# Two layer norms change engines, and the fourth block is turned one step sooner, where a mamba layer meets a linear layer

## The chip, the cores and the metric

The kernel runs on one core of one Trainium2 chip. The metric is the device time of one execution in microseconds (us). Five engines work beside each other, each on its own queue of instructions: TensorE (PE in the profile; its weight loads are PEld), VectorE (DVE), ScalarE (ACT), GpSimd (POOL) and SyncE (SP, which here issues nearly all DMA transfers). They meet through semaphores.

## The reference

Four sublayers work on x, which has 2048 tokens of 512 values. Each is added to x, and a layer norm over the 512 values follows.

```python
x = layernorm(x + mamba(x, W_in, conv, A_log, ..., W_out))   # gated scan, 16 heads of 64, state 16
x = layernorm(x + linear(x, weight, scale))     # x @ ternary weight * scale, row length bounded by tanh
x = layernorm(x + recurrent(x, w_y, w_x, conv, w_ig, w_ag, w_out))       # gelu branch times gated scan
x = layernorm(x + swiglu(x, gate, up, down))                             # 512 -> 2048 -> 512
# layernorm: (x - mean) / sqrt(var + 1e-5)
# linear: out = (x @ W) * scale; n = |out|; out *= tanh(n) / n; out *= min(0.99 / |out|, 1)
```

Everything is float32. In the linear layer the kernel writes each operand as a sum of two float32r pieces, so that one product becomes two faster ones.

## The kernel before

The tokens are worked in four blocks of 512 (`NBLK` = 4, `TB` = 512). A block lies in SBUF as `X[b]`, 128 partitions by four row groups j of 512 values. In the mamba layer the tiles of the four blocks share three buffers of the pool `outer`; block 3 gets the buffer of block 0.

The source is written as Python generators whose steps are woven together. The order of the source gives each instruction its priority; a scheduler then orders each engine's queue, taking the earliest instruction in the source that it believes ready. Each queue is strictly in order once it is made. `keep_in_program_order` holds one instruction behind all that its engine was given before it in the source.

**The end of mamba.** `conclude(3)` multiplies block 3 by `w_out` (L764), adds the result to `X[3]` (L779), calls `layernorm(X[b])` (L783) and stores the block to the DRAM tensor `x_mid` (L784, on SP). Its steps are woven with `linear(0)` and `linear(1)`. Then `first_layer.close` gives up the pool `outer`, and SP loads block 3 from `x_mid` into the tile that later layers use (L1002).

**The layer norm** (`layernorm`, L274 to L287). Its statistics are always on VectorE: `bn_stats` (L279), `bn_aggr` (L280), then a square root on ScalarE (L282) and a reciprocal (L283) on VectorE. Only the last part, four `tensor_scalar` over 128x512 (L285), one for each j, runs on the engine that is passed in. Before the change `conclude` gives VectorE for all blocks, and `linear` gives GpSimd for all blocks.

**The linear layer** (`linear(b)`) has four steps: turn the block with TensorE (L237), whose result ScalarE copies into the first piece `wu0` (L241) while VectorE makes the second piece `wd0` (L244); products of rows j = 0, 1 (L961, scaled on VectorE at L965); products of j = 2, 3; then the bound by tanh (L971 to L983), the addition to x (L985), the layer norm, and from block 1 on a store to `x_lin` (L254). There is one buffer for each piece, so a block can be turned into them only when the products of the block before it are done. For block 2 the copies of L241 are held in source order on ScalarE.

**The start of the recurrent layer.** `branches(0)` turns block 0 (L237), ScalarE copies it to `xT` (L248), and products with `w_x` (four, L1040) and `w_y` (four, L1040) follow. Its nine steps are woven with the eight of `linear(2)` and `linear(3)` by a plan that says how many of those follow each step. `xT` is a tile of the pool `rec`, which is opened on the same side of SBUF as `outer`, after `outer` is closed. In the compiled kernel `xT` takes bytes 151456 to 159648 of each partition, and `X[3]` of the mamba layer had bytes 153568 to 161760. ScalarE's first copy into `xT` therefore carries a wait for the store L784 to have landed.

Of the kernel before, what the change touches and what calls it, by code (L numbers as in the profile page):

```python
# [37 lines left out]
def model_kernel(ctx: ExitStack, tc: tile.TileContext, t: dict, out: bass.AP):  # L38
    nc = tc.nc
    ctx.enter_context(nc.allow_non_contiguous_dma(reason="small parameter columns"))  # L40
    BATCH, SEQ, _ = t["L0_attn_hidden_states"].shape
    NBLK = BATCH * SEQ // TB
# [17 lines left out]
    def bank(name):  # L60
        return ps.tile([P, 512], F32, tag="mm", name=name)
# [17 lines left out]
    def tokens():  # L79
        return op.tile([P, NJ, D], F32, tag="x", name="x", bufs=3)  # L80

    X = [tokens() for _ in range(3)]
# [170 lines left out]
    def store_rows(rows, x):  # L253
        nc.sync.dma_start(rows.rearrange("(j p) d -> p j d", p=P), x)  # L254
# [13 lines left out]
    def turn_blocks(dst, src=None, pinned=False):  # L268
        for k in range(NK):
            turned = nc.vector.transpose(dst[:, k, :], (src or dst)[:, k, :])  # L270
            if pinned:
                tc.keep_in_program_order(turned)

    def layernorm(x, n=NJ, engine=nc.vector):  # L274

        mv = sp.tile([P, NJ, 2], F32, tag="mv", name="mv")
        for j in range(n):
            st = sp.tile([P, 6], F32, tag="st", name="st", bufs=4)
            nc.vector.bn_stats(st, x[:, j, :])  # L279
            nc.vector.bn_aggr(mv[:, j, :], st)  # L280
        rs = sp.tile([P, NJ, 1], F32, tag="rs", name="rs")
        nc.scalar.activation(rs[:, :n], mv[:, :n, 1:2], AF.Sqrt, bias=eps)  # L282
        nc.vector.reciprocal(rs[:, :n], rs[:, :n])  # L283
        for j in range(n):
            engine.tensor_scalar(  # L285
                x[:, j, :], x[:, j, :], mv[:, j, 0:1], rs[:, j, :], ALU.subtract, ALU.mult
            )  # L287

    def causal_conv(acc, xpad, w, pinned=False):

        for k in range(3):
            tap = nc.vector.scalar_tensor_tensor(  # L292
                acc, xpad[:, k : k + TB], w[:, k : k + 1], acc, ALU.mult, ALU.add
            )
            if pinned and k == 0:
                tc.keep_in_program_order(tap)

    def weave(main, fill, plan, rest=True):

        for i, _ in enumerate(main):  # L300
            for _ in range(plan[i] if i < len(plan) else 0):
                next(fill, None)
        for _ in fill if rest else ():
            pass
# [451 lines left out]
    def conclude(b, st):  # L756


        xc, sums = st["xc"], st["sums"]
        rms = sp.tile([P, NJ], F32, tag="rms", name="rms")  # L760
        for j in range(NJ):
            po = bank("po")
            for m in range(NX):
                nc.tensor.matmul(  # L764
                    po, xc[:, m, j * P : (j + 1) * P], w_out[:, m, :],
                    start=(m == 0), stop=(m == NX - 1),
                )
                if m == NX // 2 - 1:
                    yield
            if j == 0:  # L770
                pss = bank("pss")
                for i in range(NJ):
                    nc.tensor.matmul(
                        pss[:, i : i + 1], sums[:, i * P : (i + 1) * P], ones,
                        start=True, stop=True,
                    )
                nc.scalar.activation(rms, pss[:, :NJ], AF.Sqrt, bias=eps, scale=1.0 / DI)
                nc.vector.reciprocal(rms, rms)
            nc.vector.scalar_tensor_tensor(  # L779
                X[b][:, j, :], po, rms[:, j : j + 1], X[b][:, j, :], ALU.mult, ALU.add  # L780
            )
            yield
        layernorm(X[b])  # L783
        nc.sync.dma_start(x_mid[b], X[b])  # L784

    def by_blocks(b, st):
# [4 lines left out]
    H, before, st = None, None, {}  # L791
# [10 lines left out]
    for b in range(NBLK):  # L802
# [19 lines left out]
        before, st = st, coming  # L822
# [43 lines left out]
    def later_layers(exact, last=None):  # L866
# [4 lines left out]
        X = Y  # L871
# [70 lines left out]
        def coming_block(b):  # L942

            x = ep.tile([P, NK, TB], F32, tag="lo", name=f"lin{b}" + suffix)
            load_blocks(x, x_lin[b])
            return x

        def linear(b):


            xT = transposed(
                ep, b, X, tags=("wu0", "wd0") if exact else ("wu0",), split=exact, behind=b == 2
            )
            yield
            o = ep.tile([P, NJ, D], F32, tag="wF", name="o" + suffix)
            ssq = sp.tile([P, NJ], F32, tag="ssq", name="ssq")
            for j in range(NJ):
                po = bank("po")
                for k in range(NK):
                    for x in xT:  # L960
                        nc.tensor.matmul(  # L961
                            po, x[:, k, j * P : (j + 1) * P], wf[:, k, :],
                            start=(k == 0 and x is xT[0]), stop=(k == NK - 1 and x is xT[-1]),
                        )
                nc.vector.tensor_tensor(o[:, j, :], po, f0s, ALU.mult)  # L965
                junk = ep.tile([P, GW], mybir.dt.bfloat16, tag="junk", name="junk2")
                nc.scalar.activation(junk, o[:, j, :], AF.Square, accum_out=ssq[:, j : j + 1])
                if j % 2:
                    yield
            norm = sp.tile([P, NJ], F32, tag="norm", name="norm")  # L970
            nc.scalar.activation(norm, ssq, AF.Sqrt)  # L971
            v = sp.tile([P, NJ], F32, tag="v", name="v")
            nc.vector.tensor_scalar(v, norm, 1e-7, None, ALU.max)
            f = sp.tile([P, NJ], F32, tag="f", name="f")
            nc.scalar.activation(f, v, AF.Tanh)
            nc.vector.tensor_scalar(v, v, 1e-7, None, ALU.add)
            nc.vector.reciprocal(v, v)
            nc.vector.tensor_tensor(f, f, v, ALU.mult)
            nc.vector.tensor_tensor(norm, norm, f, ALU.mult)
            nc.vector.tensor_scalar(norm, norm, 1e-7, None, ALU.max)  # L980
            nc.vector.reciprocal(norm, norm)
            nc.vector.tensor_scalar(norm, norm, 0.99, 1.0, ALU.mult, ALU.min)
            nc.vector.tensor_tensor(f, f, norm, ALU.mult)  # L983
            for j in range(NJ):
                nc.vector.scalar_tensor_tensor(  # L985
                    X[b][:, j, :], o[:, j, :], f[:, j : j + 1], X[b][:, j, :],
                    ALU.mult, ALU.add,
                )
            layernorm(X[b], engine=nc.gpsimd)
            if b:  # L990
                store_rows(x_lin[b], X[b])
            yield
# [40 lines left out]
        with tc.tile_pool(name="rec" + suffix, bufs=1, side="right", reuse_waits="tile") as rp:  # L1033
# [12 lines left out]
            def branches(b, st):  # L1046

                if b:
                    xT = rp.tile([P, NK, TB], F32, tag="xT", name=f"xT{b}")
                    turn_blocks(xT, lin.pop(0))  # L1050
                    if b + 1 < NBLK:
                        lin.append(coming_block(b + 1))
                else:
                    xT = transposed(rp, b, X, by_act=True)[0]
                yield
                cv = st["cv"] = rp.tile([P, NK, TB], F32, tag="cv", name="cv", bufs=2)
                y = st["y"] = rp.tile([P, NK, TB], F32, tag="y", name="y", bufs=2)
                for m in range(NK):
                    pm = product(0, m, xT)
                    xpad = rp.tile([P, 3 + TB], F32, tag="xpad", name="xpad1", bufs=2)  # L1060
                    if b % BPS == 0:
                        nc.gpsimd.memset(xpad[:, 0:3], 0.0)
                    else:
                        nc.gpsimd.tensor_copy(xpad[:, 0:3], carry[:, m, :])
                    nc.scalar.activation(xpad[:, 3:], pm, AF.Identity, bias=bx[:, m : m + 1])
                    if b % BPS < BPS - 1:
                        nc.gpsimd.tensor_copy(carry[:, m, :], xpad[:, TB : TB + 3])
                    nc.vector.tensor_scalar(
                        cv[:, m, :], xpad[:, 3:], cw1[:, m, 3:4], cb1[:, m : m + 1],
                        ALU.mult, ALU.add,  # L1070
                    )
                    causal_conv(cv[:, m, :], xpad, cw1[:, m, :])
                    yield
                for m in range(NK):
                    pm = product(1, m, xT)
                    nc.scalar.activation(y[:, m, :], pm, AF.Gelu, bias=by[:, m : m + 1])
                    yield
# [75 lines left out]
                yield  # L1153

            st = {}
            weave(branches(0, st), itertools.chain(linear(2), linear(3)), (1,) * 8)
            lin = [coming_block(1)]
            bout = row("L1_attn_b_out", D, c1, nc.sync, "scale")
            wg, wu, wd = ([weights(ep, which, 0)] for which in ("wg", "wu", "wd"))
# [255 lines left out]
```

## Time and profile before

| what | value |
|---|---|
| median of 3 runs | 1124.24 us (1123.46 to 1125.34) |
| the profiled execution | 1125.59 us, of which the span is 1123.8 us |
| TensorE | busy 98% of the span |
| VectorE, ScalarE, GpSimd | busy 62%, 41%, 32% |
| end of the mamba layer, linear layer, start of the recurrent layer | about 400 to 510 us of the span |
| TensorE's mean granted clock | 0.997 of full speed |

A busy share is of the whole span and hides stages with different limits. A row of the timeline gives the start and the length in us, the engine, the line, what is written from what, how many instructions were merged, and in brackets how long the engine stood idle before it and what ended that wait.

### The profile page before, as it was taken

Reading aid. Unit: us, or ns where it says so; the run is one execution under the profiler, and the core shown is the slowest. Engines: PE = TensorE matmul, PEld = TensorE weight load, DVE = VectorE, ACT = ScalarE, POOL = GpSimd, SP = SyncE. Lnnn points to the kernel's source line nnn. Section 1 sums busy time; section 2 is a strip of 40 time slices with the busy share of each in tenths; the row PEclk is TensorE's granted clock in tenths of the full one; section 3 lists DMA queues with packets and bytes.
Section 4 is the critical chain, followed back from the end, with each engine's and each line's share of the span. In section 5 each row is a group of like instructions: output and inputs, shape, how many; then the busy total and the mean of one; then the engine's idle time right before and its main releaser. Section 6 shows DMA issues by size and latency. Waiting matters only on the chain.

```text
span 1123.8 us, 12100 instructions
## 1 busy us (share of the span) xinstructions
PE 1104.9 (98%) x4466; PEld 666.1 (59%) x4466; DVE 698.9 (62%) x1262; ACT 455.7 (41%) x694; POOL 362.1 (32%) x347
## 2 busy tenths in 40 slices
PE   9999999999999999999999999999999999999996
PEld 5455445445544555654444444447888888888885
DVE  5979897697869676873626528174238765325224
ACT  3334633463454233556745372553223224224223
POOL 1547471465248240456123222236411001001000
PEclk9999999999999999999999999999999999999999
DMA  8005202800220038147230001303645003100001
GB/s 323 19 12 120 91 1 91 206 1 38 92 94 0 39 137 248 76 82 180 48 37 1 37 1 38 38 0 122 201 99 75 1 1 63 13 1 25 13 1 41
DMA packets 110732, 75.99 MB, mean 68 GB/s; under 512 B 86257, under 2 KB 87057, under 8 KB 108105
## 3 DMA queue, kind: packets, MB, share of 16 engines
q1 hardware_dynamic: 109464, 74.72, 24.8%
q8 instruction: 37, 0.61, 0.2%
q10 hardware_dynamic: 976, 0.39, 0.1%
q14 instruction: 31, 0.25, 0.1%
q0 software_dynamic: 224, 0.02, 0.0%
HBM read 58.91 MB, written 16.02 MB: 67 GB/s over the span
## 4 chain that ended last, share of the span: by engine, by line
PE 80%; DVE 12%; ACT 4%; issue 2%; POOL 1%; DMA 1%; SPq 0%; DVEq 0%; ACTq 0%; POOLq 0%
PE pgu L1014 20%; PE p L1040 17%; PE po L1238 10%; PE pg L366 9%; PE px L366 7%; PE po L764 6%; PE po L1128 2%; PE py L699 2%; DVE L L572 2%; DVE acc L292 2%; PE po L961 2%; DVE st L279 1%; PE pxt L668 1%; POOL x L1134 1%; DVE x L985 1%
## 5 line engine op out<-in xcount | busy, mean ns | idle before, releaser
L1025 DVE SCALAR_TENSOR_TENSOR h<-pgu,L_ffn_up_scale,sg 128x512 f32<-128x512 f32 x63 | 47.2, 749 | 127.6 <-PE pgu L1014 123.9
L764 PE MATMUL po<-w_out,xc 128*128 128x512 f32 x256 | 114.2, 600 | 2.2 <-DVE L L572 2.2
L366 PE MATMUL px<-xT,w_in 128*128 128x512 f32 x256 | 114.6, 597 | 0.0
L587 POOL TENSOR_TENSOR L<-L,gm 128x512 f32<-128x512 f32 x64 | 93.0, 1482 | 64.9 <-DVE bdec L582 38.3
L366 PE MATMUL pg<-xT,w_in 128*128 128x512 f32 x256 | 113.5, 594 | 0.0
L1040 PE MATMUL p<-xT,w 128*128 128x512 f32 x256 | 112.1, 592 | 0.6 <-ACT xT L248 0.6
L1040 PE MATMUL p<-cv,w 128*128 128x512 f32 x256 | 110.5, 592 | 0.0
L1014 PE MATMUL pgu<-wF__4250,wg 128*128 128x512 f32 x256 | 101.7, 397 | 0.0
L1014 PE MATMUL pgu<-lo__4251,wg 128*128 128x512 f32 x256 | 100.8, 394 | 0.0
L1014 PE MATMUL pgu<-lo__4251,wu 128*128 128x512 f32 x256 | 100.7, 393 | 0.0
L1014 PE MATMUL pgu<-wF__4250,wu 128*128 128x512 f32 x256 | 100.7, 393 | 0.0
L1238 PE MATMUL po<-wd,hh 128*128 128x512 f32 x252 | 98.3, 396 | 0.3 <-POOL wg L910 0.3
L1238 PE MATMUL po<-wd,hl 128*128 128x512 f32 x252 | 98.3, 396 | 0.2 <-DVE hl L1029 0.2
L1024 ACT ACTIVATE sg<-pgu,L_ffn_gate_scale 128x512 f32<-128x512 f32 x63 | 43.3, 688 | 127.7 <-PE pgu L1014 127.6
L764 PEld LDWEIGHTS po<-w_out,xc 128*128 128x128 f32 x256 | 49.0, 192 | 64.4 <-issue 57.1
L1040 PEld LDWEIGHTS p<-cv,w 128*128 128x128 f32 x256 | 48.6, 190 | 61.2 <-issue 59.6
L1028 ACT CAST hh<-h 128x512 fp32r<-128x512 f32 x63 | 39.1, 621 | 112.6 <-DVE h L1025 112.4
L1040 PEld LDWEIGHTS p<-xT,w 128*128 128x128 f32 x256 | 48.4, 190 | 58.0 <-issue 55.0
L366 PEld LDWEIGHTS px<-xT,w_in 128*128 128x128 f32 x256 | 47.5, 190 | 57.5 <-issue 55.9
L366 PEld LDWEIGHTS pg<-xT,w_in 128*128 128x128 f32 x256 | 47.3, 190 | 54.2 <-issue 53.3
L292 DVE SCALAR_TENSOR_TENSOR acc<-xpad,cols,acc 128x512 f32<-128x512 f32 x72 | 67.1, 934 | 18.9 <-ACT acc L336 14.1
L1356 POOL TENSOR_TENSOR x<-x,r 128x512 f32<-128x512 f32 x12 | 15.2, 1293 | 195.7 <-DVE r L1355 195.7
(288 smaller groups left out, 1924.8 us busy)
## 6 DMA issues: line engine op xcount, KB each, us to landing
L<-decays SPq DMA_DIRECT2D x12, 1024.0 KB, 7.0
x_mid<-x SPq DMA_DIRECT2D x4, 1024.0 KB, 3.8
x<-x_mid SPq DMA_DIRECT2D x4, 1024.0 KB, 6.8
st<-in_L_ffn_gate_w_dram SPq DMA_DIRECT2D x8, 512.0 KB, 4.1
st<-in_L_ffn_up_w_dram SPq DMA_DIRECT2D x8, 512.0 KB, 4.9
st<-in_L_ffn_down_w_dram SPq DMA_DIRECT2D x8, 512.0 KB, 4.5
x_rec<-x SPq DMA_DIRECT2D x4, 1024.0 KB
x<-_attn_hidden_states_dram SPq DMA_DIRECT2D x3, 1024.0 KB
```

The source lines that it names most:

```text
L292: tap = nc.vector.scalar_tensor_tensor(acc, xpad[:, k : k + TB], w[:, k : k + 1], acc, ALU.mult, ALU.add)
L366: nc.tensor.matmul(pm[:n, :], w_in[:, k, lo : lo + n], xT[:, k, :], start=(k == 0), stop=(k == NK - 1),)
L572: nc.vector.tensor_tensor_scan(L[:, h, :], pl, id4.rearrange("p j t -> p (j t)"), 0.0, ALU.mult, ALU.add)
L587: nc.gpsimd.tensor_tensor(L[:, h, :], L[:, h, :], st["gm"], ALU.mult)
L699: nc.tensor.matmul(pys[i][hh * HD : (hh + 1) * HD, q, :], dtx[q][:, 2 * i + hh, :], L[:, h, s], start=(first and q == 0), stop=(q == 1), s ...
L764: nc.tensor.matmul(po, xc[:, m, j * P : (j + 1) * P], w_out[:, m, :], start=(m == 0), stop=(m == NX - 1),)
L1014: nc.tensor.matmul(pm, w[g][:, k, cols], x[:, k, :], start=(k == 0 and x is pieces[0]), stop=(k == NK - 1 and x is pieces[-1]),)
L1024: nc.scalar.activation(sg, pgu[0], AF.Silu, scale=gs[:, m : m + 1])
L1025: nc.vector.scalar_tensor_tensor(h, pgu[1], us[:, m : m + 1], sg, ALU.mult, ALU.mult)
L1028: nc.scalar.copy(halves[0], h)
L1040: nc.tensor.matmul(pm, w1[i][:, k, m * P : (m + 1) * P], rhs[:, k, :], start=(k == 0), stop=(k == NK - 1),)
L1238: nc.tensor.matmul(po[j], x[:, j * P : (j + 1) * P], wd[m // GK][:, m % GK, :], start=(m == 0 and x is h[0]), stop=(m == NF - 1 and x is h ...
```

## The change

Block 3's last mamba layer norm is normalised on GpSimd instead of VectorE; block 0's norm after the linear layer on VectorE instead of GpSimd. In the plan of the weave, the step that turns block 3 for the linear layer moves from behind the fourth product with `w_x` to behind the third; the two product steps of block 3 stay behind the first and second product with `w_y`, so one more step lies between turn and products.

```diff
@@ conclude
-        layernorm(X[b])
+        layernorm(X[b], engine=nc.gpsimd if b == NBLK - 1 else nc.vector)
         nc.sync.dma_start(x_mid[b], X[b])
@@ linear
-            layernorm(X[b], engine=nc.gpsimd)
+
+            layernorm(X[b], engine=nc.gpsimd if b else nc.vector)
             if b:
                 store_rows(x_lin[b], X[b])
@@ later_layers
             st = {}
-            weave(branches(0, st), itertools.chain(linear(2), linear(3)), (1,) * 8)
+            weave(
+                branches(0, st), itertools.chain(linear(2), linear(3)), (1, 1, 1, 2, 0, 1, 1, 1)
+            )
```

## The prediction

> **What bounds the kernel now.** I read the page first, then TensorE's waits, then the timelines of the engines between 400 and 510 us, where all three edits lie.
>
> ```profile
> PE 1104.9 (98%) x4466; PEld 666.1 (59%) x4466; DVE 698.9 (62%) x1262; ACT 455.7 (41%) x694; POOL 362.1 (32%) x347
> ...
> PE 80%; DVE 12%; ACT 4%; issue 2%; POOL 1%; DMA 1%; SPq 0%; DVEq 0%; ACTq 0%; POOLq 0%
> ```
>
> TensorE is busy 98% of the span and makes 80% of the chain that ended last. None of the edits removes a matmul, so they can act only through the gaps between matmuls. From 503 us on TensorE runs without a gap until the next layer, and what is lost or won before that stays lost or won. The gaps are these.
>
> ```profile
> 459.63 3.39 PE L237 MATMUL pt<-ident,x 128*128 128x128 f32 x29 [0.40 <-POOL xpad L1062]
> 463.62 3.70 PE L1040 MATMUL p<-xT,w 128*128 128x512 f32 x8 [0.61 <-ACT xT L248]
> 470.55 0.50 PE L961 MATMUL po<-wfr,wd 128*128 128x512 f32 x1 [0.20 <-DVE wd L244]
> 493.35 0.50 PE L961 MATMUL po<-wfr,wd 128*128 128x512 f32 x1 [1.09 <-DVE wd L244]
> ```
>
> The first is the turn of block 0, which waits for its norm: GpSimd's four L285 end at 459.57. The second is the first product of the recurrent layer, which waits for ScalarE's copy to `xT`. The third and fourth are the linear products of blocks 2 and 3, which wait for their second pieces on VectorE. Together 2.3 us; and some matmuls near the third and fourth are spaced wider than they need be, so about 3.0 us could be had in all.
>
> The row that decides is the second one. What ended the wait of the copy behind it?
>
> ```profile
> 459.02 0.34 SPq L784 DMA_DIRECT2D x_mid<-x  x1
> 462.92 0.34 SPq L1002 DMA_DIRECT2D x<-x_mid  x1
> ```
> ```profile
> 462.72 0.21 ACT L975 ACTIVATE f<-v 128x4 f32<-128x4 f32 x1
> 462.99 2.05 ACT L248 COPY xT<-pt 128x512 f32<-128x512 f32 x4
> ```
>
> SP stores mamba's block 3 at 459.02, and its next instruction, the load back, waits for that store to land: it issues at 462.92. The copy to `xT` starts 0.07 us later. It waits for the same landing, since `xT` lies partly on the bytes of that block. ScalarE's tanh ends at 462.93 too, so before the change the two tie, and the wait costs nothing by itself. It has no slack either.
>
> **The change part by part.** I follow one chain: reciprocal of block 3's norm, four L285, store, landing, copy to `xT`, first product.
>
> ```profile
> 455.45 0.17 DVE L283 RECIPROCAL rs<-rs 128x4 f32<-128x4 f32 x1
> 455.65 0.67 DVE L285 TENSOR_SCALAR x<-x,mv,rs 128x512 f32<-128x512 f32 x1
> ```
> ```profile
> L285 DVE TENSOR_SCALAR x<-x,mv,rs x40: 515/540/1504, 165.8 to 1036.2; 128x512 f32<-128x512 f32 x40
> L285 POOL TENSOR_SCALAR x<-x,mv,rs x20: 2061/2072/2452, 451.2 to 782.3; 128x512 f32<-128x512 f32 x20
> ```
>
> *Linear's first norm on VectorE.* Four L285 at a median of 540 ns, overlapping slightly, take about 2.0 us. They are ready when block 0's reciprocal ends at 450.9 and come earlier in the source than the four L244 for block 1 (451.49 to 453.96) and block 3's last statistics, so they push both. Block 1's first mixed product then starts about 1.3 us later than 452.21, and block 3's reciprocal about 1.5 us later than 455.45 (part of the 2.0 us is absorbed where VectorE waited 0.73 us for TensorE), so at 457.0. Block 0 is normalised at about 453 instead of 459.57, which removes the 0.40 us gap.
>
> *Mamba's last norm on GpSimd.* GpSimd's four groups of four L285 in this region took 8.41, 9.17, 8.59 and 8.24 us, mean 8.6. GpSimd is idle then, as its other norm has left. From 457.2 it ends at 465.8. The store moves behind it, takes the 3.9 us of the present one (459.02 to 462.92) and lands at 469.7. SP stands in that wait; behind it are only the load of block 3 and later stores. Copy and first product follow as now (462.92 to 463.62, 0.7 us): 470.4 instead of 463.62. **+6.8 us**.
>
> What could fill that gap? The products of `linear(2)` would, 32 records of about 0.23 us; but the copies they need (L241 of block 2) are held on ScalarE behind the copies to `xT`. `linear(3)` needs those buffers first, and the products with `w_y` need `xT` as well. Only the turns of blocks 0 and 2 are free, and they end by about 464. So TensorE stands still some 6 us.
>
> Here a rule of the Trainium skill speaks for the change. The GPSIMD Engine Reference, section 4.1 Engine selection, says that GpSimd is about half as fast for two inputs but roughly at line rate for one, and L285 has one tensor input. By that the four would take about 2.2 us as on VectorE, the store would land at 463.3, the first product start 0.4 us late, and with the gains below the sum would be -1.6 us. The trace has 2072 against 540 ns for this very instruction, 3.8 times; I take the trace.
>
> *The clock.* This trace also shows what a standstill costs afterwards.
>
> ```profile
> 142.51 8.83 PE L764 MATMUL po<-w_out,xc 128*128 128x512 f32 x16 [1.95 <-DVE L L572]
> ```
> ```profile
> 143.00:147.00 4.00, 4.00 (x7) 1.64 (x6) 3.97 (x6) 0.49 (x1) 2.89 (x3) 0.57 0.00 0
> ```
>
> After about 2 us of idleness TensorE's granted clock (the 0.57) fell to half until about 146.6, and 16 matmuls that take 6.87 us elsewhere took 8.83: 1.96 us. The skill's page TensorE: Matmul & The Clock Gate, Part 1, puts the fall after an idle window of about 3.4 us. By that, a gap of 2 to 3 us would be free; by the row it need not be. For 6 us the fall is expected, and I take **+1.9 us** from the row. Both ends: nothing, if the slow stretch passes inside the standstill; 3.9 us, if it lasts twice as long.
>
> *What comes back.* When the copies run late, VectorE has long finished block 1's addition and statistics, so block 2's second pieces follow at once. The third gap goes: 0.35 us before 470.55 (the last matmul had streamed by 470.2) and 0.46 us in six matmuls that took 1.84 us instead of 1.38. **-0.8 us.**
>
> *The turn one step sooner.* TensorE does the same 16 transposes before the fourth product with `w_x` instead of after it. The four copies (2.03 us at 486.46) and four L244 move forward by one product, 3.4 us, and get ahead of block 2's addition and statistics (486.86 to 492.7), which now delay them. The fourth gap goes: 492.11 to 493.35, **-1.2 us**. It needs block 3 to be back: stored by 469.7, load 6.8 us, 476.5, while the turn comes after 24 product records and all of block 2's products, beyond 485. Covered. The price is that VectorE gets 2.4 us of L244 earlier in a full stretch; what it delays is convolutions, which TensorE reads only near 510. The bounds are a loss of 0.5 us, if something there becomes late, and a gain of 1.5.
>
> *Other queues.* Block 1's norm on GpSimd and its store to `x_lin` come later by about what TensorE loses; the turned block is used only after 515, and TensorE itself is later by then. The 1.3 us that block 1's products lose lie inside the longer standstill and are not added.
>
> Sum: 6.8 + 1.9 - 0.8 - 1.2 = +6.7 us. The profiled execution took 1125.59 (span 1123.8 and 1.8 around it), so this execution would take 1132.3. It stands 1.35 above the median; on the median of 1124.24 the sum gives **1130.9 us**.
>
> **The rivals.**
>
> *A, mamba's statistics win (0.07).* If the queue puts block 3's last statistics ahead of block 0's norm, GpSimd could start at 451.6 (L779 ends at 450.1, then 0.6 + 0.1 + 0.3 + 0.2 and hand-over), end at 460.2, and the store land at 464.1: +1.2 us, too short for the clock to fall, and -2.0 back: 1123.4. Against it is that block 0's norm comes earlier in the source and is ready.
>
> *B, the other side: the copy to `xT` does not wait (0.03).* Everything else in the change helps TensorE: block 0 ready 6.6 us sooner, 2.7 us of L285 gone from VectorE just before its full stretch, the turn early. All four gaps would close, 3.0 us: 1121.2. It turns on one place, the landing of L784: before about 462.4 the change wins, later it loses one for one. Against it are the 0.07 us between landing and copy, and the shared bytes.
>
> *C, worse (0.12).* The list order eats the sooner turn (TensorE does it where it did, no -1.2): 1132.1. With the clock low for twice as long as well, it is 6.8 + 3.9 - 0.8 = +9.9: 1134.1. That the products of block 3 come one step later, as the change is described, the plan does not say: they stay where they were, so nothing is counted for it.
>
> **How the numbers follow.** The forecast has 0.78, A 0.07, B 0.03, C 0.12. Within the forecast the chain runs from +4.9 (no push on the reciprocal, GpSimd at 8.2) to +7.9 (GpSimd at 9.2), the clock from 0 to 3.9, the gains from 0.8 to 3.0. Low ends together give about +2.6 us, 1126.8; high ends that are likely together give 1133.6. That holds most of the forecast and half of C, and leaves out about 2 in 10. About 0.2%, 2.25 us, is what a measurement of this kernel can tell from no change. Faster by more: B and a little of A, 0.04. Within it: most of A and the low edge of the forecast, 0.08. Slower: 0.88.
>
> **What would show it.** In the changed profile: DVE L285 rows near 451 to 453 and GpSimd's four near 457 to 466; SP's L784 near 466 and L1002 near 469.7; the copy L248 right behind that; a bracket of 5 to 7 us before TensorE's first L1040, and a granted clock of about half in the few us after it; no bracket on L244 before the linear products of blocks 2 and 3. I am wrong if L248 starts well before L1002 issues, if linear products of block 2 run in the gap, or if L784 issues before 462.

## The result, and the profile after

The changed kernel took 1132.02 us, the median of 6 runs (1130.26 to 1134.77). The kernel before, run beside it, took 1124.13 us (6 runs, 1123.43 to 1125.34). The ratio is 1.0069, with a 95% interval of 1.0058 to 1.0080: slower by 7.8 us (6.5 to 9.0).

The profiled execution is the longest of the six: 1134.77 us with a span of 1133.0 and a mean granted clock of 0.990, where the other five have 0.993 to 0.995. It lies 9.18 us above the profiled execution of before. A likely reason for it lying above the median is found below.

In what follows "the stage" is the stretch from the first linear product of block 0 (the first L961 row) to the first product of the branches that reads `cv`. In before it goes from 427.78 to 509.80, 82.02 us; in after from 427.93 to 519.03, 91.10 us. That is 9.08 us more, so practically all of the difference arises there.

The page, first the engines and then the shares of the chain of work that ended last:

```profile
PE 1108.2 (98%) x4466; PEld 668.7 (59%) x4466; DVE 699.1 (62%) x1262; ACT 456.1 (40%) x694; POOL 363.8 (32%) x347
...
PE 82%; DVE 9%; ACT 4%; POOL 2%; DMA 2%; issue 1%; SPq 0%; DVEq 0%; ACTq 0%; POOLq 0%
```

The number of instructions is the same on every engine, and TensorE is still at 98%. In the chain GpSimd and the DMA queues have gained a share each: that is the norm of mamba's last block and the store behind it. TensorE's busy time has risen by 3.3 us although no matmul was added: some ran at a lower clock.

The timeline of TensorE in after, at the places of the four gaps of before (start, duration, what, and in brackets the idle time before it and what ended it):

```profile
454.19 0.73 PE L961 MATMUL po<-wfr,wd 128*128 128x512 f32 x1 [1.98 <-DVE wd L244]
472.15 6.68 PE L1041 MATMUL p<-xT,w 128*128 128x512 f32 x8 [6.25 <-ACT xT L248]
482.15 0.79 PE L961 MATMUL po<-wfr,wd 128*128 128x512 f32 x1
501.65 0.39 PE L961 MATMUL po<-wfr,wd 128*128 128x512 f32 x1
```

The third and the fourth gap are gone: no bracket stands at 482.15 or at 501.65, nor at the turn of block 0. The second has become 6.25 us, and a new one of 1.98 us stands ahead of block 1's mixed products (from there on `wu` and `wd` alternate), where before had 0.15. The eight product records behind the large gap took 6.68 us instead of 3.70.

The chain of waits of after through this place (start, duration, engine, tile, line):

```profile
454.19 4.15 PE po L961 x10
459.25 8.26 POOL x L285 x4
467.54 3.87 DMA x_mid<-x
472.15 6.68 PE p L1041 x8
```

The 454.19 row lasted 2.60 us in before (452.21, the same ten matmuls). The norm on GpSimd and the store that waits for it follow one upon the other. The timeline of ScalarE and of SP's queue shows how the store reaches TensorE:

```profile
465.51 0.21 ACT L975 ACTIVATE f<-v 128x4 f32<-128x4 f32 x1
467.54 0.34 SPq L784 DMA_DIRECT2D x_mid<-x  x1
471.43 0.34 SPq L1003 DMA_DIRECT2D x<-x_mid  x1
471.51 2.06 ACT L248 COPY xT<-pt 128x512 f32<-128x512 f32 x4 [5.79 <-DMA x_mid<-x]
```

The tie is broken: ScalarE was free at 465.72 and stood until the store of mamba's block 3 had landed. The copy starts 0.08 us after the load back is issued, and now the profile names the DMA as what ended its wait. The first product follows 0.64 us after the copy's start.

VectorE in after, from the norm of linear's block 0 to the reciprocal of mamba's block 3 (L283 at 458.97):

```profile
451.63 1.91 DVE L285 TENSOR_SCALAR x<-x,mv,rs 128x512 f32<-128x512 f32 x4
453.44 2.49 DVE L244 TENSOR_TENSOR wd<-pt,wu 128x512 fp32r<-128x512 f32 x4
...
458.36 0.69 DVE L965 TENSOR_TENSOR o<-po,L_ffn_scale 128x512 f32<-128x512 f32 x1 [2.28 <-PE po L961]
458.97 0.17 DVE L283 RECIPROCAL rs<-rs 128x4 f32<-128x4 f32 x1
```

The same L965 in before:

```profile
454.84 0.69 DVE L965 TENSOR_TENSOR o<-po,L_ffn_scale 128x512 f32<-128x512 f32 x1 [0.73 <-PE po L961]
```

The reciprocal stands behind block 1's first L965 in VectorE's queue, and that one waited 2.28 us for TensorE's products (0.73 us in before). So the reciprocal came not when VectorE had got through its extra work, but when TensorE had delivered.

Two views of the granted clock in after (stretch, length, busy time of PE, PEld, DVE, ACT and POOL with the number of instructions in parentheses, granted clock, DMA share, GB/s). First around block 1's products, then from the start of the large gap on:

```profile
454.00:456.00 2.00, 1.81 (x4) 1.43 (x5) 2.00 (x6) 0.00 (x0) 0.00 (x0) 0.57 0.00 0
456.00:458.00 2.00, 2.00 (x7) 1.57 (x6) 0.08 (x2) 0.30 (x1) 0.00 (x0) 0.58 0.00 0
```
```profile
464.00:468.00 4.00, 1.90 (x18) 1.66 (x16) 2.18 (x9) 1.68 (x3) 3.59 (x4) 0.99 0.00 0
472.00:476.00 4.00, 3.85 (x5) 1.79 (x6) 3.43 (x11) 3.52 (x8) 0.00 (x0) 0.50 0.79 262
476.00:480.00 4.00, 4.00 (x9) 1.70 (x9) 0.63 (x2) 1.12 (x2) 0.19 (x1) 0.73 0.01 4
```

The clock fell twice in this execution. The second fall is the one that was expected; the first, at 454 to 458, follows a standstill of only 1.98 us.

### The profile page after: what moved, and what is told of

It is laid out like the page before. It is cut to its first block, busy times and chain, and to the rows that moved or that the text cites. A ratio compares the mean times of both kernels' runs of the same rounds, so it can differ in the third digit from the quotient of the medians.

```text
span 1133.0 us, 12094 instructions
## 1 busy us (share of the span) xinstructions
PE 1108.2 (98%) x4466; PEld 668.7 (59%) x4466; DVE 699.1 (62%) x1262; ACT 456.1 (40%) x694; POOL 363.8 (32%) x347
## 4 chain that ended last, share of the span: by engine, by line
PE 82%; DVE 9%; ACT 4%; POOL 2%; DMA 2%; issue 1%; SPq 0%; DVEq 0%; ACTq 0%; POOLq 0%
PE pgu L1015 20%; PE p L1041 19%; PE po L1241 10%; PE pg L366 9%; PE px L366 7%; PE po L764 6%; PE po L1129 2%; PE py L699 2%; PE po L961 2%; DVE L L572 2%; DVE acc L292 1%; PE pxt L668 1%; POOL x L1135 1%; DVE st L279 1%; DMA cdec<-since 1%
## 5 line engine op out<-in xcount | busy, mean ns | idle before, releaser
L1041 PE MATMUL p<-xT,w 128*128 128x512 f32 x256 | 114.4, 605 | 6.2 <-ACT xT L248 6.2
L1041 PE MATMUL p<-cv,w 128*128 128x512 f32 x256 | 110.5, 592 | 0.0
L1041 PEld LDWEIGHTS p<-xT,w 128*128 128x128 f32 x256 | 49.5, 194 | 66.8 <-issue 57.6
L1041 PEld LDWEIGHTS p<-cv,w 128*128 128x128 f32 x256 | 48.6, 190 | 61.2 <-issue 60.0
```

The lines of the kernel that those rows point to most:

```text
L1041: nc.tensor.matmul(pm, w1[i][:, k, m * P : (m + 1) * P], rhs[:, k, :], start=(k == 0), stop=(k == NK - 1),)
```

## The experiments

The theory is that of the prediction: the store of mamba's block 3 now lands late, the copy to `xT` waits for it because of the shared bytes, TensorE stands, and its clock falls. The rivals are B (the landing is not what holds the copy, so that the change would gain), one in which the norm on VectorE is itself the loss, and one in which the clock, not the wait, is most of it. One table holds what the twelve kernels gave. The first three columns of numbers come from each one's profiled execution and are counted from the start of its stage: when SP issues the store of mamba's block 3, when the first product with `xT` starts, and the length of the stage. The fourth is the duration of the first eight product records.

| kernel | store | product | stage | 8 records | median us | ratio to before (95%) |
|---|---|---|---|---|---|---|
| before | 31.24 | 35.84 | 82.02 | 3.70 | 1124.13 | 1 |
| after | 39.61 | 44.22 | 91.10 | 6.68 | 1132.02 | 1.0069 (1.0058 to 1.0080) |
| e1_mamba_only | 41.31 | 45.92 | 92.11 | 5.50 | 1134.84 | 1.0098 (1.0083 to 1.0114) |
| e2_linear_only | 33.79 | 38.38 | 84.56 | 3.70 | 1126.47 | 1.0014 (1.0006 to 1.0022) |
| e3_turn_only | 31.26 | 35.86 | 80.63 | 3.70 | 1122.95 | 0.9994 (0.9985 to 1.0002) |
| e4_without_mamba | 33.80 | 38.39 | 83.29 | 3.70 | 1125.17 | 1.0010 (1.0002 to 1.0018) |
| e5_xt_elsewhere | 38.01 | 36.73 | 81.71 | 3.70 | 1126.04 | 1.0009 (1.0000 to 1.0017) |
| e6_before_xt_elsewhere | 31.25 | 35.68 | 81.94 | 3.70 | 1124.53 | 1.0000 (0.9992 to 1.0009) |
| e7_warm | 38.01 | 43.77 | 87.70 | 3.70 | 1130.92 | 1.0050 (1.0037 to 1.0063) |
| e8_block2_first | 38.02 | (43.81) | 82.36 | | 1125.24 | 1.0002 (0.9994 to 1.0010) |
| e9_before_block2_first | 31.24 | (42.81) | 81.33 | | 1124.15 | 0.9996 (0.9987 to 1.0004) |
| e10_half_mamba | 34.20 | 38.81 | 84.37 | 5.35 | 1127.82 | 1.0027 (1.0017 to 1.0038) |

The ratios are to runs of before on the same chip at the same time (medians 1123.83 beside e1 to e4, 1124.72 beside e5 to e8, 1124.91 beside e9 and e10). They are not the quotients of the two medians: the thirteen executions of e2, for one, lie in two groups, five at 1124.75 to 1124.97 us and eight at 1126.42 to 1126.63, so that its median says little. A loss or gain in us after "Measured" is worked out from the ratio. In e8 and e9 the products with `xT` stand behind those of block 2 by design, so their start says nothing of a wait.

### e1_mamba_only: mamba's last norm alone

```diff
 # before, in conclude
-layernorm(X[b])
+layernorm(X[b], engine=nc.gpsimd if b == NBLK - 1 else nc.vector)
```

> Only mamba's last norm goes to GpSimd. Landing theory (the store of block 3 lands late, and the copy to xT and the first product with w_x wait for it): GpSimd works block 0's norm first, to about 459.6, then block 3's to about 468; the store lands near 471.9 and the first product starts near 472.6, 9.0 us later than before. With about 2.7 us for the low clock after it and 0.8 us back at block 2's second pieces: +10.9 us, near 1135. Rival (the loss comes from linear's norm on VectorE pushing the L244 of block 1 and the statistics of block 3): near 1125, since that norm is not moved here.

Measured: 1.0098, that is +11.0 us. The timeline of e1, GpSimd's norms, the store, the load back and the first product:

```profile
449.48 17.91 POOL L285 TENSOR_SCALAR x<-x,mv,rs 128x512 f32<-128x512 f32 x8 [32.69 <-PE pt L237]
467.41 0.34 SPq L784 DMA_DIRECT2D x_mid<-x  x1
471.30 0.34 SPq L1002 DMA_DIRECT2D x<-x_mid  x1
472.02 5.50 PE L1040 MATMUL p<-xT,w 128*128 128x512 f32 x8 [10.84 <-ACT xT L248]
```

Eight L285 run in one piece on GpSimd, since linear's block 0 is still there and mamba's block 3 has to queue behind it. The store comes 10.07 us later in the stage than in before, the first product 10.08 us. The edit of mamba alone costs more than the whole change. By the ratios the three edits alone add up to 11.0 + 1.6 - 0.7 = +11.9 us (e1, e2, e3), and together they cost 7.8: the linear edit, a loss by itself, makes GpSimd free for this one.

### e2_linear_only and e3_turn_only: the other two parts

```diff
 # e2: before, in linear
-layernorm(X[b], engine=nc.gpsimd)
+layernorm(X[b], engine=nc.gpsimd if b else nc.vector)
 # e3: before, the plan
-(1,) * 8
+(1, 1, 1, 2, 0, 1, 1, 1)
```

> Only linear's first norm goes to VectorE. Landing theory: the push is real but small; block 3's reciprocal moves from 455.5 to about 459, its norm stays on VectorE, the store lands near 466.5, first product near 467.2, +3.6 us, with a standstill too short for the clock to fall there; 0.8 us back: +2.8, near 1127. Rival (VectorE's push is the loss): near 1131.

> Only the plan of the weave. Landing theory and prediction: the gap before block 3's products goes, -1.2 us, near 1122.9, and nothing else moves. Rival (the early turn crowds VectorE's full stretch): no gain or up to 0.5 us slower.

Measured: e2 1.0014 (+1.6 us), e3 0.9994, not to be told from no change by its time. In the stage e2 loses 2.54 us and e3 gains 1.39. The timelines of TensorE and VectorE in e2:

```profile
452.45 0.50 PE L961 MATMUL po<-wfr,wd 128*128 128x512 f32 x1 [1.97 <-DVE wd L244]
456.64 0.69 DVE L965 TENSOR_TENSOR o<-po,L_ffn_scale 128x512 f32<-128x512 f32 x1 [2.29 <-PE po L961]
464.58 3.70 PE L1040 MATMUL p<-xT,w 128*128 128x512 f32 x8 [0.37 <-ACT xT L248]
```

The four L285 on VectorE push block 1's second pieces, TensorE stands 1.97 us, its clock falls (0.50 granted in this trace from 454 to 456), the first L965 waits 2.29 us, and the reciprocal behind it is late. Here mamba's norm is on VectorE and still its store comes 2.55 us later, and the first product 2.54 us later: the whole loss of the stage. So the linear edit, which makes block 0 ready sooner, is a loss by itself. Whether it passes through the landing cannot be told from e2 or e4. In e2 the store lands at 463.88 and ScalarE's tanh, which needs block 1's late products, ends at 464.0: the two tie again, as in before.

### e4_without_mamba: the change with mamba's norm back on VectorE

```diff
 # after, in conclude
-layernorm(X[b], engine=nc.gpsimd if b == NBLK - 1 else nc.vector)
+layernorm(X[b])
```

> The change without its mamba part: linear's norm on VectorE and the sooner turn. Landing theory: 2.8 of the linear edit less 1.2 of the turn, +1.6 us, near 1125.7, so about 6 us of the change's 8 hang on mamba's norm. Rival (VectorE's push is the loss): near 1130.

Measured: 1.0010 (+1.1 us; stage +1.27). It is e2 and e3 together: 2.54 - 1.39 = +1.15 in the stage. Taking back this one line takes away 6.7 of the 7.8 us.

### e5_xt_elsewhere and e6_before_xt_elsewhere: the shared bytes

Here nothing is computed elsewhere or later. Only two tiles, `gx` and `ga`, are allocated ahead of `xT`, so that `xT` comes to lie two tiles of 8192 bytes higher, at byte 167840, off those of mamba's block 3. e6 is the same edit on the kernel before, as a control.

```diff
 last_h = rp.tile([P, NK], F32, tag="last", name="last")
+kept_low = {
+    tag: rp.tile([P, NK, TB], F32, tag=tag, name=tag) for tag in ("gx", "ga")
+}
...
-gx = rp.tile([P, NK, TB], F32, tag="gx", name="gx")
-ga = rp.tile([P, NK, TB], F32, tag="ga", name="ga")
+gx, ga = (
+    kept_low.pop(tag, None) or rp.tile([P, NK, TB], F32, tag=tag, name=tag)
+    for tag in ("gx", "ga")
+)
```

> The whole change, but two later tiles of the pool (gx and ga) are allocated ahead of xT, so that xT lies on bytes that mamba's block 3 never had. Landing theory: the copy to xT no longer waits for the store, though the store is as late as in the changed kernel (near 471). ScalarE's tanh ends near 465.7, the first product starts near 466.4, TensorE hardly stands still and its clock stays up: 1124.5, that is 7.5 us off the changed kernel. Rival (the loss comes from GpSimd's and VectorE's norms themselves, the landing is only late beside it): stays near 1131.

> The kernel before with xT on other bytes, as a control. Landing theory: landing and tanh tie in the kernel before, so without the wait the copy still starts behind the tanh, near 462.9: no change, 1123.8. If the new place of the tiles itself made something faster or slower, it would show here.

Measured: e5 1.0009 (+1.0 us), e6 1.0000. The timeline of e5, ScalarE's copy, the first products, the store and the load back:

```profile
464.42 2.02 ACT L248 COPY xT<-pt 128x512 f32<-128x512 f32 x4
465.04 3.70 PE L1044 MATMUL p<-xT,w 128*128 128x512 f32 x8 [0.33 <-ACT xT L248]
466.32 0.34 SPq L784 DMA_DIRECT2D x_mid<-x  x1
470.22 0.34 SPq L1003 DMA_DIRECT2D x<-x_mid  x1
```

The norm is still on GpSimd and the store still late: it comes at 466.32, which is 38.01 us into the stage against 31.24 in before, and lands at 470.22. (It is 1.60 us earlier than in after, because the clock did not fall at block 1's products in this trace.) The copy has started 5.8 us ahead of the landing. The eight records take 3.70 us again. The control shows that the other address by itself is worth nothing. So the wait of the copy for the landing is the cause, and it goes through the bytes, not through any value: with it gone, 6.8 of the 7.8 us are gone by the timed runs, and the profiled stage is 0.31 us shorter than in before. This is the experiment that decides between the theory and its rivals. It does not give the gain that B promised: it lies at +1.0 us, not at -3. The number expected for it (1124.5) was 1.5 us too low, of which some 0.5 us is the chip, since before took 1124.72 beside it. The first product comes 0.89 us later than in before, since the linear edit's push on VectorE remains: ScalarE's tanh ends at 464.51, 1.05 us later in the stage.

### e7_warm: TensorE kept busy

In after, 52 repeats of transposes of block 2 are put behind its turn (their result is what stands there already), so that TensorE works through most of the gap.

```diff
+for j in range(52 if behind and k == NK - 1 else 0):
+    tc.keep_in_program_order(nc.tensor.transpose(
+        pt[:, j % NJ * P : (j % NJ + 1) * P],
+        X[b][:, j % NJ, k * P : (k + 1) * P], ident,
+    ))
```

> The whole change, with 52 more transposes of block 2 into the bank that holds the same result (about 5.6 us at 0.107 each) behind its turn, to keep TensorE busy while the first product waits. Landing theory: the copy to xT starts as late as before, near 471.5, but the clock stays up, and the first eight product records take about 3.4 to 3.7 us instead of 6.1: about 2.7 us off the changed kernel, near 1129.3. Rival (those records are slow because ScalarE's copies feed them slowly): they stay at about 6 us, near 1132 or a little more.

Measured: 1.0050 (+5.6 us). TensorE in e7 (L241 are the added transposes, L1046 the product, L253 the copy), and the granted clock behind it:

```profile
464.86 5.84 PE L241 MATMUL pt<-ident,x 128*128 128x128 f32 x52
472.41 3.70 PE L1046 MATMUL p<-xT,w 128*128 128x512 f32 x8 [1.71 <-ACT xT L253]
```
```profile
472.00:476.00 4.00, 3.59 (x9) 1.68 (x10) 2.29 (x6) 3.98 (x9) 0.00 (x0) 1.00 0.71 262
```

The first product is nearly as late as in after (43.77 against 44.22 from the start of the stage), but the clock is full and the eight records take 3.70 us instead of 6.68. The stage is 3.40 us shorter: 2.98 from the records, 0.45 from the earlier product. So in these traces the fall of the clock after the standstill is a real part of the loss, but not the most of it. By the timed runs the part is less sure, since the intervals of after and e7 overlap (1.0058 against 1.0063). The store took 5.04 us to land in e7 (466.65 to 471.69), where after and most others have 3.9; e8 has 4.40. The transfers of e7 between 462 and 473 us show something that may bear on it:

```profile
q1 hardware_dynamic: 152, 1.11, 27.3%
q8 instruction: 1, 0.02, 0.8%
```

The columns are packets, MB and the share of 16 engines' time. A load of instructions, one packet that begins between 466.4 and 466.5 us, just ahead of the store's issue, runs on beside it; 0.8% of 16 engines for 11 us is 1.4 us of one engine. e8 has such a load within its store's time as well (0.5% of the same length, 0.9 us); none of the other ten kernels has one between 4 us ahead of the issue and the landing of this store. The excess of the landings, 1.15 and 0.51 us, goes the same way. That is suggested by the traces, not tested. If that is the cause, e7 would have come out about 1 us lower without it.

### e10_half_mamba: half of the norm on GpSimd

```diff
 # after, in layernorm: an engine for each row group
-engine.tensor_scalar(
+(engine[j] if isinstance(engine, tuple) else engine).tensor_scalar(
 # in conclude
-layernorm(X[b], engine=nc.gpsimd if b == NBLK - 1 else nc.vector)
+layernorm(X[b], engine=(nc.gpsimd,) * 2 + (nc.vector,) * 2 if b == NBLK - 1 else nc.vector)
```

> The whole change, but of mamba's last norm only two of the four row groups go to GpSimd; the other two stay on VectorE. Landing theory (the loss follows GpSimd's time one for one): GpSimd needs 4.1 us instead of 8.3, the store lands near 467.3 instead of 471.4, first product near 468.0 instead of 472.1; TensorE's standstill there shrinks from 6.2 to about 2 us, where the clock may or may not fall: 4.1 to 6.5 us off the changed kernel, 1125.5 to 1128. Rival (any use of GpSimd there costs the same, say by slowing VectorE beside it): near 1131.

Measured: 1.0027 (+3.0 us). The timelines of GpSimd, SP and TensorE, and the clock behind the gap:

```profile
456.47 4.41 POOL L285 TENSOR_SCALAR x<-x,mv,rs 128x512 f32<-128x512 f32 x2 [39.08 <-DVE rs L283]
464.80 0.34 SPq L1003 DMA_DIRECT2D x<-x_mid  x1
465.52 5.35 PE L1041 MATMUL p<-xT,w 128*128 128x512 f32 x8 [2.40 <-ACT xT L248]
```
```profile
466.00:468.00 2.00, 2.00 (x3) 0.69 (x3) 2.00 (x5) 2.00 (x5) 0.00 (x0) 0.50 0.81 303
```

The store is 2.96 us later than in before, the first product 2.97. With e2, after and e1 that makes four points (2.55, 2.96, 8.37 and 10.07 us for the store; 2.54, 2.97, 8.38 and 10.08 for the product) on a line of slope one: once the landing is the last thing, it passes on in full. In after, e1 and e10 the profile names the DMA as what ended the wait of the copy; e2's point lies on the line too, but there landing and tanh tie. The clock fell after 2.40 us of standstill too, and the eight records lost 1.65 us.

### e8_block2_first and e9_before_block2_first: work put into the gap

Block 2's turn and its linear products are put ahead of the branches' first product, and its copies are no longer held behind those to `xT`. e8 does this on after, e9 on before (with the sooner turn).

```diff
+fill = itertools.chain(linear(2), linear(3))
+for _ in range(3):
+    next(fill)
+weave(branches(0, st), fill, (0, 0, 0, 2, 0, 1, 1, 1))
...
-behind=b == 2
+behind=False
```

> The whole change, but block 2 is turned and multiplied by the linear weight before the recurrent layer's first step in the source, and its copies are not held in source order. Landing theory: the store is as late, but 7.3 us of block 2's products fill the standstill; the clock stays up; near 1123.5, at most 1125. Rival (VectorE and GpSimd are what is late): the products of block 2 would themselves wait and little is won, near 1130.

> A candidate for better than both: both norms as in the kernel before, the sooner turn of block 3, and block 2 turned and multiplied by the linear weight before the recurrent layer's first step, so that GpSimd's norm of block 0 and the landing of mamba's block 3 lie behind its 7.3 us of products. Theory: the gaps of 0.40, 0.61 and 0.8 us go and one of about 1.4 for block 2's second pieces comes, and the turn gives its 1.2: near 1122.3, 0.9987 of before. Rival: the new order only shifts the gaps, 1123.5 to 1125.

Measured: e8 1.0002, e9 0.9996. The timeline of SP and TensorE in e8:

```profile
464.64 0.34 SPq L784 DMA_DIRECT2D x_mid<-x  x1
468.68 1.91 PE L237 MATMUL pt<-ident,x 128*128 128x128 f32 x16
469.04 0.34 SPq L1003 DMA_DIRECT2D x<-x_mid  x1
470.43 10.46 PE L1041 MATMUL p<-xT,w 128*128 128x512 f32 x24
```

The store is issued 38.02 us into the stage, as late as in e5 and e7, and lands at 469.04; but TensorE has block 2's products until then, no bracket stands before the first L1041, and the whole loss is gone (+0.2 us, -0.7 to +1.1). That makes the wait harmless by covering it, where e5 did it by taking it away. On the kernel before, the same order with the sooner turn gains nothing that can be told (e9, expected about 2 us faster): its interval holds 1. Its stage is 0.69 us shorter, and e3's, without the other order, 1.39: putting block 2 first took back half of what the sooner turn had won. No kernel of this study is faster than before by a measurable amount.

## Why the prediction was right, and where its terms were off

The forecast case came true: the landing of the store of mamba's block 3 holds the copy to `xT`, and TensorE stands. Predicted was +6.7 us on the median, 1130.9; measured +7.8, 1132.02, inside the range and on the predicted side. e5 shows the wait, e4 that mamba's edit brings it, e10 and e1 how it passes on. Against the profiled execution, whose stage lost 9.08 us, the terms stand as follows.

*Reciprocal of block 3, +1.5 us: mis-sized in this execution.* It came 3.37 us later in the stage. The prediction let the 1.5 us follow from VectorE's extra work, part of which was to be absorbed in VectorE's wait for TensorE, and it said: "The 1.3 us that block 1's products lose lie inside the longer standstill and are not added". The products do not lie beside the chain. They are a link of it: the reciprocal is queued behind the first L965, which waits for those products, and the push of the second pieces makes them 1.83 us later, not 1.3. In e5, e8 and e10, whose clock stayed at 1.00 there, the reciprocal came at 29.46 to 29.48 us of the stage, 1.8 us later than in before (27.67). The first L965 of e5 and e8 still waited 0.71 and 0.70 us, against 0.73 in before, so nothing was absorbed. That 1.8 lies near the 1.5 is partly luck. In after, e2 and e4, whose clock fell to about half, the reciprocal came at 31.04 to 31.05. So the fall after the short gap is worth 1.6 us, and the prediction counted one fall of the clock where there can be two.

*GpSimd, 8.6 us: 8.26.* The four L285 took 8.26 us in after, at the short end of the range that the prediction took its mean from. Each of the four took some 2.07 us, where VectorE's four took 1.91 us together, so the row of before gave the right size, and the rule of the Trainium skill that was weighed against it (GPSIMD Engine Reference, section 4.1 Engine selection) does not hold for this instruction.

*Landing and copy, 3.9 and 0.7 us: right.* They were 3.89 (467.54 to 471.43) and 0.72 us (471.43 to 472.15). The chain without the first fall was predicted to issue the store at about 465.8, 38.0 us into the stage; e5, e7 and e8 have it at 38.01, 38.01 and 38.02. That it fits so closely is luck: 0.3 us too little on the reciprocal and 0.3 us too much on GpSimd cancel.

*The clock after the standstill, +1.9 us: mis-sized.* The eight records took 2.98 us more. The value lies between the two ends that were given, 0 and 3.9. It was taken from one row behind a gap of 2 us, where TensorE worked at half clock for 3.41 us. Half of that is 1.7 us, so 1.96 was itself a little too much: in the view that the row of 8.83 us is from, 16 such matmuls elsewhere take 7.03 us, not 6.87. In after the half clock lasted until 478.2, that is 6.0 us into the work. The last section shows why this is not a matter of the length of the gap.

*What comes back, 0.8 and 1.2 us: right, a little more.* Both brackets are gone. The start of the first product (+8.38) and the records (+2.98) make 11.36 us, and the stage lost 9.08, so 2.28 us came back. e3 shows the turn's part alone, 1.39 us of the stage.

*The rivals.* A did not occur: linear's norm ran before block 3's statistics, at 451.63. B was wrong where it mattered and right in its form: e5 removes the wait, and the loss with it. But its 1121.2 rested on the gaps alone and left out the push of linear's norm on VectorE. C has two halves: the turn was not eaten (e3), and the low clock lasted three times as long as in the row (10.24 against 3.41 us), but 4.2 us of it passed inside the standstill.

*The range.* Its ends do not follow from the terms given for them. 4.9 + 0 - 3.0 is +1.9 us, not +2.6, and GpSimd at 9.2 makes the chain +7.4, not +7.9. The result lies inside either way.

Left open: whether the five other executions of after, 1130.26 to 1132.05 us, had the first fall of the clock. Without it their sum would be 9.08 - 1.6 = +7.5 us, near the measured 7.8, but only the longest was profiled. Their mean granted clocks of 0.993 to 0.995 against 0.990 say that they ran at half clock for less time: 0.003 to 0.005 of 1131 us, doubled, gives an estimate of 7 to 11 us less, two or three stretches of 3.41 us. Which ones, the record does not show; one may lie behind the last matmuls, where the clock falls too and nothing is lost.

## What to carry to other kernels

Before an operation is moved to an idle engine, follow what it releases to the end, transfers included: here an engine with nothing to do took 8.3 us for what had taken 2.7 on VectorE, and behind it hung a 3.9 us store whose bytes another stage was waiting to overwrite. A wait that ties with another one has no slack, and a tile's address can be a dependency as hard as its value; moving the tile, or putting free work in front of it, took nearly the whole loss away. When an engine's queue holds a short instruction behind one that waits for another engine, the delay of the short one is the other engine's, not the sum of the work ahead of it.

## What the runs showed of the hardware that was not expected

The granted clock can fall after a standstill of about 2 us, and need not. The gap before block 1's products was 1.97 or 1.98 us in seven traces. Behind it the clock fell to half in after, e2 and e4, and stayed at 1.00 in e5, e7, e8 and e10. e5 has the instructions of after at other addresses, so the moment decides and not the work.

The traces show which moments these are. In the views of after above, a clock of 0.57 over 2 us means 1.72 us at half, so the clock fell at 454.28; by the same working it came back at 457.68, fell again at 467.9 and came back at 478.2. In slices of 0.1 us the four moments are 454.29, 457.70, 467.94 and 478.18: once and three times 3.41 us apart. In all twelve traces, leaving out the last 15 us of the kernel, every stretch at half clock lasted 3.41 us or, in after and e1, three times that. So the clock looks as if it were set anew every 3.41 us, at moments that the work does not choose.

What counts then is how long TensorE stood still between two such moments. The whole of the short gap of after, 452.21 to 454.19, lies between 450.87 and 454.29, and the clock fell. That of e5, 452.58 to 454.56, reaches over a moment at 454.36, only 1.77 us of it lie ahead, and the clock stayed. Over all twelve traces the clock fell after each of the eleven steps of 3.41 us at full clock that held 1.94 us of standstill or more, and after none that held 1.83 or less. It came back after steps with at most 0.06 us of standstill, and not after the one of after with 0.79. This is a rule worked out from these traces; no run was made to test it.

So what a standstill costs afterwards does not grow with its length: it is half of that part of the low stretch in which TensorE works again. Behind 2.40 us (e10) that part was 3.35 us and the eight records lost 1.65, behind 6.25 us (after) it was 6.03 and they lost 2.98, behind 10.84 us (e1) 3.65 and 1.80. This is likely part of the scatter between executions of one kernel: the two groups of e2's executions lie 1.6 us apart, which is what one fall is worth, and have mean granted clocks of 0.997 to 0.998 and of 0.996.
